# Filter products by a 52x128 block matrix in a two-layer spectral kernel, with new orders for its first two stages

## The chip, the cores and the metric

The kernel runs on one core of a Trainium2 chip. The core has TensorE (PE; its weight loads are PEld in the profile), VectorE (DVE), ScalarE (ACT) and GpSimd (POOL); SyncE (SP) issues nearly all of the DMAs, which sixteen DMA engines carry out. The metric is the device time of one launch in microseconds (us), the median of three runs.

## The reference, cut to what matters

Two layers; in each, a spectral mixing block and a feed-forward block are added to an image tensor of 8 images of 128 x 128 pixels with 96 channels. The mixing block, of which the change touches the filter part:

```
x_pre = relu(norm(x) @ w1.T) ** 2                       # 192 channels
xf    = rfft2(x_pre)                                    # 128 x 65 frequencies
filt[s] = Rh[s] @ cw[s] @ Rw[s].T                       # s = 3 scales: (16,9), (8,4), (24,13) -> (128,65), complex
comb  = sum_s softmax_s(gate(x)) * filt[s]              # an image's own mixture, for each channel
x     = x + irfft2(xf * comb) @ w2.T
```

`cw[s]` is real and imaginary, for 192 channels. Rw resizes along the width to 65 frequencies and Rh along the height to 128. Rw does not depend on the image, so its product is made once in each layer, by the code that is changed here.

## The kernel before, in words

**Work and stages.** Sixteen jobs (two layers of eight images) go through three pipelined stages, each in 16 steps for one image: P (`pixels`, 8 rows of pixels a step: norm, projection, squaring, transform along the width), F (`frequencies`, 4 width frequencies a step: transform along the height, filter, projection, inverse transform along the height) and S (`tokens`: inverse transform along the width, then the feed-forward block). P hands its result to F through the DRAM tensors `a_d`, F to S through `y_d`. F is 19 ticks behind P, S 19 behind F.

**Order.** The order of the work is written by hand. A tick goes through a table of entries (stage, step, how many items ahead), and each entry advances the generator of the stage by one `yield`. The order in the table is the program order on every engine. Ticks -5 to 14 use `RAMP` (P only), 15 to 35 `RISE` (P and F), 36 to 257 `TICK` (all three), then `FALL` and `TAIL`. For the P steps named here: 0 loads xt, 1 are the statistics (L491), 2 is the normalisation on GpSimd (L562), 3 the transposes pt_a (L566), 4 ScalarE's copy xT, 5 and 10 the projections pw0 and pw1 (L577), 6 and 11 ScalarE's r, 9 and 14 VectorE's sums sd (L595), 15 and 16 the width transforms pa0 and pa1 (L604), 17 to 20 ScalarE's lo, VectorE's at and the store to `a_d`. For the F steps: 0 loads al and ut, 1 is the filter times the image's mixture (L711, GpSimd), 2 to 4 are pf and px (L723, L739), 5 and 10 py (L757), 13 and 14 pz (L839, L847), 16 is pi (L863). N are the norm's small operations, G the gate of an image, which in RISE runs at ticks 16 and 17 for the first image and at 32 and 33 for the second.

**PSUM.** Five tags share the eight banks: d0, d1 and d2 are pairs of banks, s3 and s4 single ones. `RAMP_BANKS` and `RISE_BANKS` say which tile uses which tag in a stage. A tile waits until the one before it on its tag has been read.

**The filter products (U).** `load_filters` puts a layer's coefficients into `cw`: four blocks of 26 rows (9 + 4 + 13 width coefficients) at partitions 0, 32, 64 and 96, each for 48 channels, with 96 (real and imaginary, 48 heights) as the innermost dimension. `filters(i)` makes a group of 8 of the 96 heights: step 0 is four matmuls of 26 rows x 65 columns by 384, one in each 32-row quarter (L294), into ps_u (the pair d0) and ps_v (s3, s4); step 1 two copies on ScalarE (L307), step 2 two on VectorE (L309), step 3 a store to `u_d` (L314), which for each frequency writes a run of 8 x 192 fp32. There are 12 groups in a layer: layer 0 at ticks 3 to 14, layer 1 at ticks 21 to 32 (`UAHEAD`, `UPAUSE`). The moving operand is

```
cws[l][32 * i : 32 * i + NWS, :, n0 : n0 + UN].rearrange("p m n -> p n m")
```

which steps from channel to channel by 96 fp32. F reads `u_d` at its step 0 as ut, 112 rows of heights by 4 (or 5) frequencies.

**Background.** `background()` loads coefficients and weights, one piece a tick from tick 0, at the entry ("P", 9) of the table.

Of the kernel before, what the change touches and what calls it, by code (L numbers as in the profile page):

```python
# [1 line left out]

# [8 lines left out]
F32 = mybir.dt.float32  # L11
# [28 lines left out]
UM = 48  # L40
UN = 8
NU = NG // UN
# [3 lines left out]
EVENTS_AFTER = ("P", 9)  # L46
# [30 lines left out]
    ("U", 3, -1),    ("F", 7, 1), ("P", 1, 2), ("P", 0, 3), ("P", 13, -1), ("U", 0, 0), ("F", 12, 0),  # L77
    ("P", 3, 1), ("P", 5, 0), ("N", 0, 0), ("U", 1, 0), ("P", 4, 1), ("F", 13, 0),
    ("U", 2, 0), ("P", 14, -1), ("P", 6, 0), ("P", 15, -1), ("F", 8, 1), ("P", 16, -1),
    ("P", 17, -1), ("F", 14, 0), ("P", 7, 0), ("P", 18, -1), ("F", 9, 1), ("P", 8, 0),  # L80
    ("F", 10, 1), ("P", 19, -1), ("P", 20, -1), ("N", 1, 0), ("F", 15, 0), ("F", 11, 1),
    ("P", 9, 0), ("F", 0, 3), ("P", 10, 0), ("P", 11, 0), ("F", 16, 0), ("F", 1, 2),
    ("F", 2, 2), ("N", 2, 0), ("F", 3, 2), ("F", 17, 0), ("P", 12, 0), ("P", 2, 2),
    ("F", 4, 2), ("F", 5, 2), ("F", 18, 0), ("F", 6, 2),
# [3 lines left out]
    1: ((8, 0), (25, 1), (29, 2), (37, 3), (38, 4), (42, 5), (45, 6)),  # L88
    2: ((7, 7), (24, 8), (30, 9), (32, 10)),
# [14 lines left out]
    ("U", 3, -1), ("U", 0, 0), ("P", 0, 5), ("P", 13, 0), ("U", 1, 0), ("P", 20, -1), ("P", 7, 1),  # L104
    ("P", 1, 4), ("U", 2, 0), ("P", 3, 2), ("P", 4, 2), ("P", 8, 1), ("N", 1, -1),
    ("P", 14, 0), ("N", 0, 0), ("N", 2, -1), ("P", 2, 3), ("P", 9, 1), ("P", 10, 1),
    ("P", 15, 0), ("P", 11, 1), ("P", 16, 0), ("P", 17, 0), ("P", 18, 0), ("P", 19, 0),
    ("P", 5, 2), ("P", 12, 1), ("P", 6, 2),
# [12 lines left out]
    "pa0": 0, "pa1": 1, "pw0": 2, "pw1": 2, "pt_a": 1, "ps_u": 0, "ps_v0": 3, "ps_v1": 4,  # L121
# [8 lines left out]
    "ps_g": 3, "ph": 3, "pl": 3, "pa0": 2, "pa1": 0, "pw0": 0, "pw1": 2, "pt_a": 2,  # L130
    "pf0": 0, "pf1": 2, "py0": 1, "py1": 1, "pz0": 3, "pz1": 4, "pi0": 3, "pi1": 4,
    "px": 3, "pg": 3, "ps_u": 0, "ps_v0": 3, "ps_v1": 4,
# [35 lines left out]
def _constants():  # L168
# [48 lines left out]
    rw4 = np.zeros((128, NKW))  # L217
    for i in range(M // UM):
        rw4[32 * i : 32 * i + NWS] = rw
    made = dict(  # L220
        dft=f_w, fwd=np.stack(fwd, 1), inv=np.stack(inv, 1), idft=d, rh=rh2, rw=rw4,
# [18 lines left out]
def metaformer_kernel(ctx: ExitStack, tc: tile.TileContext, x, cst, layers, out):  # L240
# [33 lines left out]
    u_d = [dram.tile([NKW, GP, M], F32, name=f"u_d{l}") for l in range(len(layers))]  # L274
# [4 lines left out]
    def load_filters(l, p):  # L279

        cws[l] = us.tile([128, UM, NG], F32, name="cw")
        for i in range(M // UM):
            if l and i:
                yield
            nc.sync.dma_start(cws[l][32 * i : 32 * i + NWS], p["cw"][:, i * UM : (i + 1) * UM, :])

    def filters(i):

        l, n0 = i // NU, i % NU * UN
        pu = bank2("ps_u")  # L290
        pss = [pu[:NKW, i, : UN * UM] for i in range(2)]
        pss += [bank1(f"ps_v{i}")[:NKW, : UN * UM] for i in range(2)]
        for i in range(M // UM):
            mm(  # L294
                pss[i].rearrange("p (n m) -> p n m", m=UM),
                kt["rw"][32 * i : 32 * i + NWS],
                cws[l][32 * i : 32 * i + NWS, :, n0 : n0 + UN].rearrange("p m n -> p n m"),
                start=True,
                stop=True,
            )  # L300
        yield
        u = us.tile([NKW, UN, M], F32, name="u", bufs=3)
        uv = u.rearrange("p n (i m) -> p i n m", m=UM)
        for i, ps in enumerate(pss):
            o = ps.rearrange("p (n m) -> p n m", m=UM)
            if i < 2:
                nc.scalar.copy(uv[:, i], o)  # L307
            else:
# [784 lines left out]
```

## Time and profile before

| | |
|---|---|
| median of three runs | 4905.85 us (4905.08 to 4906.21) |
| profiled execution, its own time | 4904.48 us |
| its span, first to last instruction | 4901.7 us |
| granted TensorE clock, mean | 0.987 |
| start of the projection pw of tiles 0, 16, 32 | 20.84, 137.88, 391.92 us |
| ticks with U: ramp, rise (the usual one) | 7.33, 16.08 us |
| ticks without U: ramp, rise (the usual one) | 6.28, 14.32 us |
| DMA share: 50 to 137, 137 to 182, 196 to 392 us | 74%, 85%, 69% |
| L294, records and median | 192, 0.82 us |
| L307 (ScalarE), L309 (VectorE) | 48 x 0.48, 48 x 0.55 us |

A tick's length is read from TensorE's timeline, from one block of transposes (pt_a) to the next. A record's duration includes its way through the array, so the distance from one start to the next tells what a matmul costs, and not its duration. An fp32 matmul stands in the records twice. "Idle before" in square brackets names what ended the wait.

### The profile page before, as it was taken

What the parts mean: (1) busy time and instruction counts of PE and PEld (TensorE: products, weight loads), DVE (VectorE), ACT (ScalarE), POOL (GpSimd) and SP (SyncE); (2) the same over time, 40 slices, a digit from 0 to 9 for tenths busy, and PEclk for the clock granted to TensorE, in tenths of its full rate; (3) what the DMA queues carried; (4) which work ended last, traced back from release to release, by engine and by line L of the source; (5) the groups of instructions that cost most, each with busy time, mean ns of one, the idle gap of its engine ahead of it and who ended that gap; (6) DMA issues with size and microseconds to landing.
All of it is one profiled execution on the core that took longest, in us unless ns stands there. A gap on an engine that the chain in (4) does not pass through costs nothing.

```text
span 4901.7 us, 123978 instructions
## 1 busy us (share of the span) xinstructions
PE 4811.2 (98%) x44232; PEld 3752.2 (77%) x44232; DVE 4595.1 (94%) x13949; ACT 4314.8 (88%) x7104; POOL 2535.4 (52%) x1886
## 2 busy tenths in 40 slices
PE   8999999999999999999999999999999999999997
PEld 5677787777777777777877777777777777777764
DVE  8888999999999999999999999999999999998998
ACT  7555999999999999999999999999999999998987
POOL 4444555555555555555555555555555555554544
PEclk9999999999999999999999999999999999999997
DMA  6767777777777777777777777877777777776754
GB/s 196 206 188 210 206 215 214 215 212 216 212 213 215 217 215 214 213 214 215 216 213 215 213 216 212 219 213 213 213 214 214 212 219 213 214 215 180 207 169 125
DMA packets 917424, 1020.95 MB, mean 208 GB/s; under 512 B 75826, under 2 KB 848914, under 8 KB 916602
## 3 DMA queue, kind: packets, MB, share of 16 engines
q1 hardware_dynamic: 916810, 1013.04, 74.7%
q8 instruction: 352, 5.77, 0.5%
q14 instruction: 262, 2.15, 0.1%
HBM read 598.92 MB, written 413.84 MB: 207 GB/s over the span
## 4 chain that ended last, share of the span: by engine, by line
PE 89%; DVE 5%; ACT 4%; issue 1%; DMA 0%; POOL 0%; SPq 0%; POOLq 0%; DVEq 0%; ACTq 0%
PE pw L577 17%; PE py L757 14%; PE pz L847 9%; PE pf L723 7%; PE pa L604 7%; PE pi L863 7%; PE pm L942 6%; PE pz L839 5%; PE po L959 5%; PE pt_a L566 5%; PE ps_r L897 4%; PE pt_c L932 2%; DVE st L491 1%; ACT y L945 1%; ACT xn_c L918 1%
## 5 line engine op out<-in xcount | busy, mean ns | idle before, releaser
L800 POOL TENSOR_TENSOR xf<-pr 128x768 f32<-128x768 f32 x512 | 932.0, 1820 | 422.4 <-DVE pr L785 402.1
L577 PE MATMUL pw<-w,xT 97*128 97x240 f32 x4096 | 942.5, 373 | 6.1 <-DVE at L621 3.5
L757 PE MATMUL py<-k_fwd,al 128*128 128x128 f32 (+1 forms) x6208 | 801.8, 280 | 0.0
L945 ACT CAST y<-pm 128x1024 f16<-128x1024 f32 x768 | 754.4, 1017 | 42.0 <-PE pm L942 41.7
L577 PEld LDWEIGHTS pw<-w,xT 97*128 97x128 f32 x4096 | 741.4, 191 | 59.3 <-ACT r L580 10.9
L757 PEld LDWEIGHTS py<-k_fwd,al 128*128 128x128 f32 (+1 forms) x6208 | 744.6, 191 | 40.6 <-DVE pr L785 2.5
L952 ACT ACTIVATE h<-a 128x1024 fp8e5<-128x1024 f16 x729 | 773.3, 1061 | 0.2 <-DVE a L948 0.2
L589 POOL TENSOR_TENSOR acc<-acc,r 128x192 f32<-128x192 f32 x496 | 296.6, 598 | 919.0 <-ACT r L580 835.9
L977 POOL TENSOR_TENSOR y<-xr,o 128x768 f32<-128x768 f32 x256 | 422.2, 1649 | 671.4 <-DVE o L974 598.2
L580 ACT ACTIVATE r<-pw 128x960 f32<-128x960 f32 x512 | 497.3, 971 | 127.0 <-PE pw L577 127.0
L781 DVE TENSOR_TENSOR pr<-py,cf 128x768 f32<-128x768 f32 x512 | 488.1, 953 | 55.7 <-PE py L757 41.1
L595 DVE TENSOR_TENSOR sd<-xs 128x384 f32<-128x384 f32 x1008 | 522.8, 560 | 0.7 <-issue 0.3
L711 POOL TENSOR_TENSOR ut<-ut,rw 112x768 f32<-112x768 f32 (+1 forms) x256 | 473.3, 1849 | 41.0 <-DMA ut<-u_d 30.7
L723 PEld LDWEIGHTS pf<-k_rh,ut 48*128 48x128 f32 x6080 | 362.5, 189 | 149.2 <-issue 141.3
L942 PE MATMUL pm<-xq,f_q 96*128 96x512 fp8e5 x1536 | 432.1, 391 | 28.7 <-ACT y L945 22.7
L562 POOL TENSOR_TENSOR xn_a<-xt,n_rs 128x768 f32<-128x768 f32 x256 | 382.2, 1493 | 133.6 <-DVE n_rs L525 120.6
L935 ACT ACTIVATE xq<-pt_c 96x1024 fp8e5<-96x1024 f32 x256 | 261.2, 1020 | 202.0 <-PE pt_c L932 202.0
L583 ACT ACTIVATE xs<-r 128x768 f32<-128x768 f32 x512 | 436.8, 853 | 0.4
L723 PE MATMUL pf<-k_rh,ut 48*128 48x128 f32 x6080 | 412.0, 282 | 4.3 <-POOL ut L711 3.3
L918 ACT ACTIVATE xn_c<-xr,n_nb,n_rs 128x96 fp8e5<-128x96 f32 x1058 | 413.1, 487 | 0.0
L847 PE MATMUL pz<-w2c,xf 128*128 128x96 f32 x2048 | 396.6, 275 | 0.0
L764 ACT COPY cf<-pf 128x768 f32<-128x768 f32 x496 | 372.9, 801 | 26.6 <-PE pf L723 26.3
(133 smaller groups left out, 10173.6 us busy)
## 6 DMA issues: line engine op xcount, KB each, us to landing
a_d<-at SPq DMA_DIRECT2D x256, 768.0 KB
al<-a_d SPq DMA_DIRECT2D x1024, 192.0 KB
y_d<-yt SPq DMA_DIRECT2D x512, 192.0 KB
v<-y_d SPq DMA_DIRECT2D x256, 384.0 KB
ut<-u_d SPq DMA_DIRECT2D x256, 336.0 KB
xt<-in_x_dram SPq DMA_DIRECT2D x512, 96.0 KB
xr<-in_x_dram SPq DMA_DIRECT2D x256, 192.0 KB
mid<-y SPq DMA_DIRECT2D x256, 192.0 KB
```

Of the source, the lines that this page charges most:

```text
L577: mm(o, xT[:, 4 * a + 2 * i + j, :], wt["w1"], start=True, stop=True)
L580: nc.scalar.activation(r.rearrange("p a s c -> p a (s c)"), pw, AF.Relu)
L595: on.tensor_tensor(sd[:, e], xs[:, 0], xs[:, 1], op)
L711: nc.gpsimd.tensor_tensor(ut[:, -n:], ut[:, -n:], _bc_mid(jb.rw, n), ALU.mult)
L723: mm(pf[:, i, t * 128 : (t + 1) * 128], utf[64 * i : 64 * i + NHS, c0 : c0 + 128], kt["rh"][64 * i : 64 * i + NHS, :], start=True, stop=True,)
L757: mm(py[p0:p1, t, e, :], alf[:, e, c0 + p0 : c0 + p1], f, start=True, stop=True)
L781: nc.vector.tensor_tensor(p0, yv, crb, ALU.mult)
L800: nc.gpsimd.tensor_tensor(xf.rearrange("p t e f -> p (t e) f"), pr[:, 0].rearrange("p t r k -> p t (r k)"), pr[:, 1].rearrange("p t r k -> ...
L847: mm(pz[t][:, j, e, :], xf[:, 2 * t, e, :], wt["w2c" if t else "w2a"], start=False, stop=j == e == 1,)
L942: mm(pm[:, s, :], fk, xq[:, s, :], start=True, stop=True)
L945: nc.scalar.copy(y16, pm)
L952: nc.scalar.activation(hk, a16, AF.Copy, saturate=False)
```

## The change

- `cw` now holds 52 rows in each half of the partitions: the 26 rows of channels 0 to 95 and, below them, the 26 rows of channels 96 to 191. Both halves (partitions 0 to 51 and 64 to 115) hold the same coefficients, so each layer's coefficients are loaded twice. The constant rw becomes a block matrix: 52 x 128, of 2 x 64 frequencies.
- A group is 4 heights, real in the lower half and imaginary in the upper: two matmuls of 52 rows x 128 columns by 384, into ps_v0 and ps_v1; one copy on ScalarE, one on VectorE, both of 128 partitions; two stores of runs of 96 fp32. There are still 12 groups in a layer, in the same ticks.
- The 65th frequency (index 64) needs only the last coefficient of each scale. `load_filters` loads these in six pieces, transposes them (two transposes, one ScalarE copy) and stores them to `u_d`.
- `u_d` has 128 rows for each frequency, not 112.
- RAMP and RISE have new orders, banks and gate places; in RISE the xt loads are 4 ahead, not 3. The background starts at tick -3, at the entry ("P", 12); the weights of layer 1 are loaded two kinds at a time.

```diff
-UM = 48
-UN = 8
-NU = NG // UN
+UN = 4
+NU = NHS // UN
-EVENTS_AFTER = ("P", 9)
+EVENTS_AFTER = ("P", 12)
...
 RISE = (
-    ("U", 3, -1),    ("F", 7, 1), ("P", 1, 2), ("P", 0, 3), ("P", 13, -1), ("U", 0, 0), ("F", 12, 0),
-    ("P", 3, 1), ("P", 5, 0), ("N", 0, 0), ("U", 1, 0), ("P", 4, 1), ("F", 13, 0),
-    ("U", 2, 0), ("P", 14, -1), ("P", 6, 0), ("P", 15, -1), ("F", 8, 1), ("P", 16, -1),
-    ("P", 17, -1), ("F", 14, 0), ("P", 7, 0), ("P", 18, -1), ("F", 9, 1), ("P", 8, 0),
-    ("F", 10, 1), ("P", 19, -1), ("P", 20, -1), ("N", 1, 0), ("F", 15, 0), ("F", 11, 1),
-    ("P", 9, 0), ("F", 0, 3), ("P", 10, 0), ("P", 11, 0), ("F", 16, 0), ("F", 1, 2),
-    ("F", 2, 2), ("N", 2, 0), ("F", 3, 2), ("F", 17, 0), ("P", 12, 0), ("P", 2, 2),
-    ("F", 4, 2), ("F", 5, 2), ("F", 18, 0), ("F", 6, 2),
+    ("P", 1, 2), ("P", 13, -1), ("F", 12, 0), ("P", 14, -1), ("F", 7, 1), ("P", 3, 1),
+    ("N", 0, 0), ("P", 5, 0), ("P", 4, 1), ("P", 6, 0), ("U", 0, 0), ("U", 1, 0),
+    ("P", 15, -1), ("P", 16, -1), ("U", 2, 0), ("F", 13, 0), ("F", 8, 1), ("F", 14, 0),
+    ("P", 17, -1), ("P", 7, 0), ("U", 3, -1), ("F", 9, 1), ("P", 18, -1), ("P", 8, 0),
+    ("P", 19, -1), ("P", 20, -1), ("F", 0, 3), ("F", 10, 1), ("N", 1, 0), ("P", 0, 4),
+    ("F", 11, 1), ("P", 9, 0), ("F", 15, 0), ("P", 10, 0), ("N", 2, 0), ("F", 16, 0),
+    ("P", 11, 0), ("F", 1, 2), ("F", 2, 2), ("F", 17, 0), ("F", 3, 2), ("F", 18, 0),
+    ("P", 12, 0), ("P", 2, 2), ("F", 4, 2), ("F", 5, 2), ("F", 6, 2),
 )
 RISE_GATE = {
-    1: ((8, 0), (25, 1), (29, 2), (37, 3), (38, 4), (42, 5), (45, 6)),
-    2: ((7, 7), (24, 8), (30, 9), (32, 10)),
+    1: ((4, 0), (29, 1), (29, 2), (43, 3), (44, 4), (46, 5), (46, 6)),
+    2: ((16, 7), (28, 8), (30, 9), (33, 10)),
 }
...
 RAMP = (
-    ("U", 3, -1), ("U", 0, 0), ("P", 0, 5), ("P", 13, 0), ("U", 1, 0), ("P", 20, -1), ("P", 7, 1),
-    ("P", 1, 4), ("U", 2, 0), ("P", 3, 2), ("P", 4, 2), ("P", 8, 1), ("N", 1, -1),
-    ("P", 14, 0), ("N", 0, 0), ("N", 2, -1), ("P", 2, 3), ("P", 9, 1), ("P", 10, 1),
-    ("P", 15, 0), ("P", 11, 1), ("P", 16, 0), ("P", 17, 0), ("P", 18, 0), ("P", 19, 0),
-    ("P", 5, 2), ("P", 12, 1), ("P", 6, 2),
+    ("P", 19, -1), ("P", 0, 5), ("P", 13, 0), ("P", 1, 4), ("P", 7, 1), ("P", 20, -1),
+    ("N", 1, -1), ("P", 8, 1), ("N", 0, 0), ("P", 14, 0), ("N", 2, -1), ("P", 15, 0),
+    ("U", 0, 0), ("P", 3, 2), ("U", 1, 0), ("P", 4, 2), ("P", 9, 1), ("P", 10, 1),
+    ("P", 5, 2), ("P", 16, 0), ("P", 17, 0), ("P", 11, 1), ("P", 18, 0), ("U", 2, 0),
+    ("P", 12, 1), ("P", 6, 2), ("U", 3, 0), ("P", 2, 3),
 )
...
 RAMP_BANKS = {
-    "pa0": 0, "pa1": 1, "pw0": 2, "pw1": 2, "pt_a": 1, "ps_u": 0, "ps_v0": 3, "ps_v1": 4,
+    "pa0": 0, "pa1": 1, "pw0": 2, "pw1": 1, "pt_a": 2, "ps_v0": 4, "ps_v1": 3,
 }
 RISE_BANKS = {
-    "ps_g": 3, "ph": 3, "pl": 3, "pa0": 2, "pa1": 0, "pw0": 0, "pw1": 2, "pt_a": 2,
+    "ps_g": 4, "ph": 4, "pl": 3, "pa0": 2, "pa1": 0, "pw0": 0, "pw1": 2, "pt_a": 2,
...
-    "px": 3, "pg": 3, "ps_u": 0, "ps_v0": 3, "ps_v1": 4,
+    "px": 3, "pg": 4, "ps_v0": 3, "ps_v1": 4,
 }
...
-    rw4 = np.zeros((128, NKW))
-    for i in range(M // UM):
-        rw4[32 * i : 32 * i + NWS] = rw
+    rw2 = np.zeros((128, 128))
+    for h in range(2):
+        for i in range(2):
+            p = 64 * h + NWS * i
+            rw2[p : p + NWS, 64 * i : 64 * i + 64] = rw[:, :-1]
...
-    u_d = [dram.tile([NKW, GP, M], F32, name=f"u_d{l}") for l in range(len(layers))]
+    u_d = [dram.tile([NKW, 128, M], F32, name=f"u_d{l}") for l in range(len(layers))]
...
     def load_filters(l, p):
-        cws[l] = us.tile([128, UM, NG], F32, name="cw")
-        for i in range(M // UM):
-            if l and i:
+        cws[l] = us.tile([128, C, NG], F32, name="cw")
+        for i in range(2):
+            for h in range(2):
+                q = 64 * h + NWS * i
+                nc.sync.dma_start(cws[l][q : q + NWS], p["cw"][:, C * i : C * i + C, :])
                 yield
-            nc.sync.dma_start(cws[l][32 * i : 32 * i + NWS], p["cw"][:, i * UM : (i + 1) * UM, :])
+        last = us.tile([C, 2, NG], F32, name="cw_last")
+        h0 = w0 = 0
+        for h, w in SCALES:
+            w0 += w
+            to = last.rearrange("p u (r n) -> p u r n", r=2)[:, :, :, h0 : h0 + h]
+            end = p["cw"][w0 - 1].rearrange("(u p) (r n) -> p u r n", u=2, r=2)
+            for u in range(2):
+                nc.sync.dma_start(to[:, u], end[:, u, :, h0 : h0 + h])
+            h0 += h
+        yield
+        ps = bank1("ps_w")[:NG, :M]
+        for u in range(2):
+            nc.tensor.transpose(ps[:, u * C : (u + 1) * C], last[:, u], ident[:C, :C])
+        ends = us.tile([NG, M], F32, name="cw_end")
+        nc.scalar.copy(ends, ps)
+        yield
+        for r in range(2):
+            nc.sync.dma_start(u_d[l][NKW - 1, 64 * r : 64 * r + NHS, :], ends[NHS * r : NHS * r + NHS])
 
     def filters(i):
         l, n0 = i // NU, i % NU * UN
-        pu = bank2("ps_u")
-        pss = [pu[:NKW, i, : UN * UM] for i in range(2)]
-        pss += [bank1(f"ps_v{i}")[:NKW, : UN * UM] for i in range(2)]
-        for i in range(M // UM):
+        pss = [bank1(f"ps_v{h}")[:, : UN * C] for h in range(2)]
+        for h, ps in enumerate(pss):
+            q, n1 = slice(64 * h, 64 * h + 2 * NWS), NHS * h + n0
             mm(
-                pss[i].rearrange("p (n m) -> p n m", m=UM),
-                kt["rw"][32 * i : 32 * i + NWS],
-                cws[l][32 * i : 32 * i + NWS, :, n0 : n0 + UN].rearrange("p m n -> p n m"),
+                ps.rearrange("p (n m) -> p n m", m=C),
+                kt["rw"][q],
+                cws[l][q, :, n1 : n1 + UN].rearrange("p m n -> p n m"),
                 start=True,
                 stop=True,
             )
         yield
-        u = us.tile([NKW, UN, M], F32, name="u", bufs=3)
...
+        u = us.tile([128, 2, UN * C], F32, name="u", bufs=3)
+        nc.scalar.copy(u[:, 0], pss[0])
+        yield
+        nc.vector.tensor_copy(u[:, 1], pss[1])
+        yield
+        for b in range(2):
+            dst = u_d[l][:64, :, C * b : C * b + C].rearrange("k (h n) m -> k h n m", h=2)
+            nc.sync.dma_start(
+                dst[:, :, n0 : n0 + UN],
+                u[64 * b : 64 * b + 64].rearrange("p h (n m) -> p h n m", m=C),
+            )
         yield
...
     def background():
+        constants("rw")
         yield from load_filters(0, layers[0])
-        constants("rw")
-        yield
         yield from other_weights(0, layers[0])
...
         for k, _ in enumerate(token_weights(0, layers[0])):
-            if k >= 3:
+            if k >= 1:
                 next(cw1)
             yield
-        for _ in cw1:
-            yield
-        yield
+        yield from cw1
         yield from projection_weights(1, layers[1])
-        yield from other_weights(1, layers[1])
-        yield from token_weights(1, layers[1])
+        for _ in zip_longest(other_weights(1, layers[1]), token_weights(1, layers[1])):
+            yield
...
-        ud = u_d[jb.l].rearrange("k n m -> n k m")
+        ud = u_d[jb.l].rearrange("k n m -> n k m")[:GP]
...
-                    if t >= 0:
+                    if t >= -3:
                         next(events, None)
```

## The prediction

> **What bounds the kernel now.** I read the page's busy table first, then TensorE's and VectorE's timelines in the first 60 us and at 420 us, the table of stretches, the tile view of the filter products, and SyncE's waits. The page says that TensorE sets the time:
>
> ```profile
> PE 4811.2 (98%) x44232; PEld 3752.2 (77%) x44232; DVE 4595.1 (94%) x13949; ACT 4314.8 (88%) x7104; POOL 2535.4 (52%) x1886
> ```
>
> The change touches the two first stages only: the ramp (ticks -5 to 14, to about 138 us) and the rise (ticks 15 to 35, to about 455 us). The filter products (group U, L294) run at ticks 3 to 14 and 21 to 32, once each. TensorE's timeline, a ramp tick without U and one with it:
>
> ```profile
> 37.89 1.05 PE L566 MATMUL pt_a<-ident,xn_a 128*96 128x128 f32 x8 [0.42 <-DVE at L621]
> ...
> 44.17 1.05 PE L566 MATMUL pt_a<-ident,xn_a 128*96 128x128 f32 x8 [0.34 <-DVE at L621]
> 45.06 1.79 PE L577 MATMUL pw<-w,xT 97*128 97x240 f32 x8
> 46.77 1.52 PE L604 MATMUL pa<-sd,dft 64*64 64x384 f32 x16
> 48.23 1.89 PE L577 MATMUL pw<-w,xT 97*128 97x240 f32 x8
> 50.04 0.84 PE L294 MATMUL ps_u<-cw,k_rw 26*65 26x384 f32 x2
> 50.06 0.84 PE L294 MATMUL ps_v<-cw,k_rw 26*65 26x384 f32 x2
> 50.71 0.82 PE L294 MATMUL ps_u<-cw,k_rw 26*65 26x384 f32 x2
> 50.72 0.82 PE L294 MATMUL ps_v<-cw,k_rw 26*65 26x384 f32 x2
> 51.47 1.08 PE L566 MATMUL pt_a<-ident,xn_a 128*96 128x128 f32 x8
> ```
>
> Each fp32 matmul leaves two records, so a group's eight are four matmuls side by side: the second pass starts 0.67 us after the first, and the block holds TensorE 1.43 us (50.04 to 51.47). The table of stretches, two ramp ticks (without, with U) and two rise ticks (with, without U); after the length come PE, PEld, DVE, ACT, POOL busy, clock, DMA share:
>
> ```profile
> 37.89:44.17 6.28, 5.94 (x40) 4.20 (x41) 6.02 (x25) 5.51 (x11) 3.92 (x5) 1.00 0.81 234
> 51.47:58.80 7.33, 7.33 (x53) 4.41 (x49) 6.89 (x25) 6.25 (x12) 3.89 (x5) 1.00 0.64 204
> ...
> 211.43:227.51 16.08, 16.08 (x137) 12.11 (x133) 13.38 (x35) 9.30 (x17) 7.94 (x6) 1.00 0.45 133
> ...
> 422.36:436.68 14.32, 14.32 (x126) 11.87 (x125) 12.59 (x34) 8.44 (x15) 8.11 (x7) 1.00 0.85 236
> ```
>
> So U costs 1.05 us in a ramp tick (without it VectorE is the bound, TensorE idles 0.34 to 0.42) and 1.76 in a rise tick, where TensorE has no gap. All of U is worth 12 x 1.05 + 12 x 1.76 = 33.7 us: that caps the gain.
>
> **What the skill says.** Trainium skill, SBUF — State Buffer, section Door 1: an SBUF line is 16 bytes, and a stream reads at full rate only with two or more hits in a line, so fp32 may step by four elements at most. U's moving operand steps by 96 floats from element to element, before and after. The trace agrees: at the same 384 columns, pa (L604, contiguous, four tiles side by side) takes 1.45 us for four passes, some 0.33 us a pass, U takes 0.67, twice as long. TensorEngine Tiling (Array Packing), Key Properties, says that a change of tiling mode drains the array: py takes 1.44 us to the next start when pt_a follows in the same mode (420.92 to 422.36) and 1.53 when U does (208.47 to 210.00), so a switch costs 0.09; and pt_a and the pw after it together take 0.24 longer behind U. The forecast goes by the trace's sizes and the pages' reasons. The trace alone can't exclude that four row tiles at once make U slow, and not the stride; that is the first rival.
>
> **Part by part.**
>
> *The products.* Two 52-row matmuls take the place of four 26-row ones that already ran side by side. Columns (384) and stride are the same, so the passes are too: 2 x 0.66 = 1.32 us. Nothing is saved in the stream. Weights are 128 columns, not 65: the load rows are 0.19 (as pf's) and 0.13, +0.06 if exposed.
>
> *Order in the rise.* U stood between py and pt_a, two modes of its own (1.76 - 1.32 = 0.44 of switching and slower first records). It now stands between pw and pa, which switched anyway, in the same 64-row halves as pz and pf: one switch more, 0.09. So 1.32 + 0.06 + 0.09 = 1.47 for 1.76: -0.29 a tick, x12 = -3.5 us.
>
> *Order in the ramp.* pa1, pa0, U, pt_a, pw, pw: three switches instead of four, -0.1 to -0.2, against +0.06 of weights. 7.33 becomes about 7.2: x12 = -1.6. VectorE's tick without U is 6.28; two copies, 0.47 apart, made that 7.2, and one makes it 6.75, no longer close to TensorE. Three ticks from 70 to 94 us last 7.52, 7.97 and 8.22, where VectorE's memsets and TensorE's waits for it meet; with the room -1.
>
> *Evictions.* One ScalarE copy less (0.48) and one VectorE copy less (0.55) a group. In the rise they stood beside a full TensorE (VectorE 13.4 of 16.1): worth nothing. The pair of banks of ps_u is freed; no wait for it shows.
>
> *A new wait.* In the rise pw0 and pa1 share bank pair 0, and pa0, pa1 now follow pw0 with only U between. pa1 must wait for ScalarE's r: 0.97 us that begins 0.1 after pw0, against pa0's 0.73. With U (1.4) it is hidden; in the ticks without U it leaves 0.4 of a bubble, and pz, py and all of TensorE stand behind it. Six such full ticks (18 to 20, 33 to 35): +2.4.
>
> *The 65th frequency.* A layer: two transposes (0.11 each in pt_a), one 96x192 copy (0.3), six loads of short runs and two stores (SyncE 0.4 each, 3 us in three ticks). TensorE reaches the transposes a tick after the loads. Less than 1 us in all, put at 0; if the loads are later than a tick, some 2 us a layer.
>
> *DMA.* Each layer's filter coefficients are loaded twice, once for each row half: as much again as the 104 rows of 18.4 KB, which took 1.26 us each, so 104 x 1.26 / 16 = 8 us more of every engine in each layer. In layer 0 they go out from tick -3 in four pieces rather than in one burst at 25.8 us; in layer 1 at ticks 15 to 18, where the DMA share is 84% (137 to 182 us) and GpSimd waits 2.6 us for a ut's load (L711). Against that, al and ut are issued earlier in a tick, before the piece and before xt, where they stood behind both. SyncE: xt now stands behind F0's al and ut loads and the at store, but it is issued a tick earlier. At the change of stage the ticks' chains differ (the gate's steps move, xT before pa0 on one bank pair): I put +1, from -4 to +6, because idle TensorE there runs slower for a while (pa 2.84 us at 143.23 for 1.45).
> u's stores were 65 rows of 6 KB a group, 0.25 us each: 65 x 0.25 / 16 = 1.0 us of each engine. Now they are 1024 runs of 384 B. The trace has only loads of that size, 22 ns each: 1024 x 22 / 16 = 1.4 us, the lower bound; the upper is the second rival's. I take the row's 22, and then the stores are hidden: the DMA engines are 64% to 77% busy in these ticks.
>
> *Sum.* -3.5 - 1.6 - 1 + 2.4 + 1 = -2.7 us. The profiled execution took 4904.48 (span 4901.7, 2.8 around it), the median is 4905.85; both less 2.7 gives 4901.8 and 4903.1. Forecast 4903. From tick 36 on nothing is changed but u_d's row pitch; that part, nine tenths of the time, stays.
>
> **Rivals.**
>
> *Four tiles, not the stride, made U slow.* Then two tiles run at pa's rate, 0.66 for two passes instead of 1.32: rise -0.66 x 12 = -7.9; ramp only to VectorE's 6.75, -0.45 x 12 = -5.4. 4903 - 13.3 = 4890. For it: no other strided operand is in the trace to compare. Against it: the factor is two, just what one hit a line for two gives, and pa too has more than one tile.
>
> *The ramp becomes bound by the stores (slower).* Trainium skill, DMA: Bandwidth & Descriptors, Specifications: below 512 B a transfer is a read-modify-write. No run here shows its price. In the ramp the stores of at and the loads of xt take 3.65 us of each engine a tick (128 x 292 ns and 512 x 41 ns, over 16), the constants 0.75; of a 7.2 us tick 2.8 is left: 44 ns a run is the point from which it decides. The 768 B rows reach 60 to 70 when crowded; at 65 the runs take 4.2 us, and the twelve ticks 1.4 more each (3.65 + 0.75 + 4.2 = 8.6 for 7.2), +17. With the ramp's gain gone: 4922. In the rise (69% of 16 us busy) 3 us more still fit. Three buffers of u give three ticks of delay before ScalarE's copy waits.
>
> *A worse order than I see* at the change of stage, where each idle spell also slows TensorE: +6 beyond the sum, 4909, still within what counts as no change.
>
> **How the numbers follow.** 0.2% is 9.8 us, about what a measurement of this kernel can tell from no change. Stride stays the limit and the DMA hides: 0.66, at 4903, its own range 4895 to 4911 (the change of stage -4 to +6, the three ticks, the weights); I leave it 0.12 of this beyond -9.8 and 0.06 beyond +9.8. Full rate: 0.16, 4890. Stores bind or loads of the second layer hold the rise up: 0.18, 4912 to 4925. Faster 0.08 + 0.15 = 0.23, rounded to 0.25; slower 0.04 + 0.16 = 0.20, to 0.22; the rest 0.53. The range takes in the full-rate case and most of the slow one: 4887 to 4918.
>
> **What would show it.** Right: U's passes still 0.66 apart; a block of about 1.4 us; ramp ticks with U 7.1 to 7.25, TensorE without gap; rise ticks with U 15.7 to 15.9; those without U 14.6 to 14.8 with a gap before pa that ScalarE's r ends; the end of the rise about 3 us earlier. Wrong: passes 0.33 apart (the first rival); ScalarE's u copies waiting for u's stores, VectorE for xt, the DMA share near 1 in the ramp (the second); or a different tick after 455 us, which none of the steps explains.

## The result, and the profile after

| | before | changed |
|---|---|---|
| median of 13 runs each, the same chip | 4906.41 us (4903.09 to 4911.13) | 4917.36 us (4914.37 to 4920.56) |
| profiled execution, its own time | 4904.48 us | 4918.25 us |
| its span, granted clock | 4901.7 us, 0.987 | 4916.2 us, 0.986 |

The ratio is 1.0022, with a 95% interval from 1.0015 to 1.003: the change costs 11 us. The forecast was 4903, three microseconds less than before. The time lies inside the range that was given (to 4918), but in the case "slower by over 0.2%", which had a chance of 0.22.

TensorE is still the busiest engine, and its busy time is as before within 1.1 us:

```profile
PE 4812.3 (98%) x44140; PEld 3756.1 (76%) x44140; DVE 4591.5 (93%) x13925; ACT 4306.3 (88%) x7082; POOL 2532.5 (52%) x1886
```

So the 11 us are not more work for TensorE; the stretches below show where it idles and where it runs slower. To find the place I took the start of each tile's first width transform (pa) from both traces and subtracted. The difference stays at 12.1 us from tile 38 to tile 60 and is 12.0 at the last tile: from about 500 us on nothing is slower in sum. (The last 420 us, after the last pa, are the same code in every kernel here and took between 418.2 and 425.1 in the profiled executions, with no pattern. Spans therefore differ by up to 7 us for no reason that this study looks at, and stretches are compared instead.) What lies ahead of tile 60:

| stretch, by pa's start | before | changed | difference | by ticks | the forecast's steps |
|---|---|---|---|---|---|
| up to tile 0 (tick 0) | 34.13 | 31.84 | -2.3 | +0.8 | not treated |
| tiles 0 to 5 (ticks 0 to 5): the first ticks of the ramp | 34.62 | 40.20 | +5.6 | +6.5 | nothing but shorter U ticks |
| tiles 5 to 14 (ticks 5 to 14): the rest of the ramp | 67.68 | 65.78 | -1.9 | -1.9 | -1.6 and -1, over twelve ticks |
| tiles 14 to 19 (ticks 14 to 20): the change of stage | 62.81 | 72.25 | +9.4 | +6.4 | +1, and +0.4 for each tick without U |
| tiles 19 to 31 (ticks 20 to 32): rise with U | 195.56 | 193.90 | -1.7 | -1.5 | -3.5 |
| tiles 31 to 35 (ticks 32 to 36): the last U tick, then rise without U | 63.64 | 66.47 | +2.8 | +1.9 | +1.2 |
| tiles 35 to 60 (ticks 36 to 61) | 458.16 | 458.30 | +0.1 | -0.2 | 0 |

**Where the cut falls.** pa's start is not the same point of the work in the two orders. In a tick of the old ramp, U, pt_a and pw1 stand ahead of pa0; in the new ramp pa0 stands ahead of them. At tile 14 the changed kernel therefore still has a U (1.47 us), a pt_a (0.9) and a pw (1.7) to do that the kernel before has behind it, and at tile 19 only the first pz (1.06). Some 3 of the 9.4 us are this, and not a loss. The column "by ticks" has the difference from the first TensorE instruction of a tick's table to that of another's; a tick's table holds the same TensorE steps in both orders, so up to there both kernels have done the same work. Everything said of the change of stage across the two orders goes by this column: it takes 69.66 us for 63.21, 6.4 more.

The table of stretches for ticks 0 to 3 and 14 to 20, before and changed in turn, says how the time is lost:

```profile
31.03:50.04 19.01, 18.00 (x121) 12.57 (x119) 17.09 (x63) 16.67 (x30) 11.48 (x13) 1.00 0.75 205
31.84:57.65 25.81, 21.21 (x124) 15.10 (x123) 18.28 (x70) 16.82 (x30) 11.21 (x12) 0.87 0.75 176
132.38:195.59 63.21, 53.56 (x390) 40.64 (x390) 48.83 (x152) 35.66 (x63) 27.84 (x25) 0.89 0.79 193
137.82:207.48 69.66, 58.98 (x388) 44.32 (x381) 49.08 (x149) 35.46 (x63) 26.13 (x24) 0.80 0.93 226
```

After the length come PE's busy time and, in the third place from the end, its granted clock. Of the 6.8 us lost in ticks 0 to 3, TensorE idles 3.6 longer and is busy 3.2 longer with the same work, at a clock of 0.87 for 1.00. At the change of stage it idles only 1.0 longer and is busy 5.4 longer, at 0.80 for 0.89. So of these 13.2 us the larger part, 8.6, is TensorE running slower and the smaller part is idle time. In the whole run this doesn't show, because its busy time is shorter elsewhere (by 2.9 us in ticks 20 to 32 alone).

**The steady ticks** are near where the forecast put them. This is TensorE's timeline of the changed kernel, a ramp tick:

```profile
111.35 1.08 PE L581 MATMUL pt_a<-ident,xn_a 128*96 128x128 f32 x8
112.27 3.41 PE L592 MATMUL pw<-w,xT 97*128 97x240 f32 x16
115.61 1.52 PE L619 MATMUL pa<-sd,dft 64*64 64x384 f32 x16
117.06 1.54 PE L314 MATMUL ps_v<-cw,k_rw 52*128 52x384 f32 x4
118.53 1.08 PE L581 MATMUL pt_a<-ident,xn_a 128*96 128x128 f32 x8
```

U's block takes 1.47 us (117.06 to 118.53), near what the four small matmuls took (1.43), and the tick is 7.18 us (111.35 to 118.53). The table of stretches shows this ramp tick from pa on, then a rise tick with U and one without:

```profile
113.89:121.06 7.17, 7.17 (x45) 4.59 (x44) 6.92 (x24) 6.04 (x12) 3.89 (x4) 1.00 0.85 257
239.80:255.59 15.79, 15.79 (x130) 12.17 (x129) 12.85 (x34) 8.92 (x16) 7.93 (x7) 1.00 0.81 209
434.61:449.48 14.87, 14.55 (x127) 11.77 (x126) 12.51 (x33) 8.32 (x15) 8.10 (x7) 1.00 0.68 178
```

The first two have no gap in TensorE. The third has 0.32 us of it, and TensorE's timeline names the place: between the two pa of a tile, and it is ScalarE's r that ends it, as the forecast said of pa1.

```profile
436.32 0.88 PE L619 MATMUL pa<-sd,dft 64*64 64x384 f32 x8
437.51 0.88 PE L619 MATMUL pa<-sd,dft 64*64 64x384 f32 x8 [0.32 <-ACT r L595]
438.32 1.14 PE L854 MATMUL pz<-w2b,xf 64*128 64x96 f32 x16
```

In the kernel before the two pa stand in one block:

```profile
426.02 1.52 PE L604 MATMUL pa<-sd,dft 64*64 64x384 f32 x16
427.47 0.46 PE L847 MATMUL pz<-w2a,xf 128*128 128x96 f32 x2
```

From the first pa to the pz behind them it is 2.00 us, for 1.45: all of the 0.55 that the tick is longer (14.87 for 14.32) lies here.

**The start.** From tile 1 to tile 2 the changed kernel takes 12.89 us, the kernel before 6.28. The chain of waits of the changed kernel (start, length, what) runs through two DMAs there:

```profile
17.75 13.16 DMA cw<-in_L_cw_dram
...
30.93 10.48 DMA xt<-in_x_dram
...
41.51 0.72 DVE st L506 x4
...
44.07 6.44 PE pw L592 x16
```

A coefficient load issued at 17.75 lands 13.16 us later. SyncE waits for that before it issues the next piece of a tile's pixels (xt, at 30.93), which takes 10.48 us to land behind another such load. VectorE's statistics start on it at 41.51, its copies of at stand behind them, and TensorE's pw, which waits for these, then runs at a granted clock of 0.54 (6.44 us; 3.4 in the steady ticks). The table of waits (total, times, longest) shows the same twice, for VectorE and for SyncE's queue:

```profile
DVE st L506 <- DMA xt<-in_x_dram: 13.4, 4, 6.0
```

```profile
SPq L567 <- DMA cw<-in_L_cw_dram: 13.6, 3, 5.7
```

In the kernel before, VectorE has no wait for xt there, and SyncE's only waits for cw are short (1.2 and 0.7) and in front of other transfers:

```profile
SPq L624 <- DMA cw<-in_L_cw_dram: 1.2, 1, 1.2
```

From 14 to 50 us the DMA table gives the queue's share of the 16 engines as 86.3% in the changed kernel and 63.8% before. The bytes, 6.48 MB for 6.11, differ by only 6%, because other transfers have been pushed out of the stretch (16 issues of xt for 24). By size, the 104 rows of coefficients of layer 0 take 2.98 us each, 19.4 us of every engine, for 1.37 us and 8.9 before (layer 1: 18.7 for 7.5). The last of them ends at 46.6 us.

**The change of stage.** Here the chain of the changed kernel is again made of DMAs:

```profile
152.27 8.41 DMA a_d<-at
...
164.03 4.42 DMA xt<-in_x_dram
168.45 1.78 POOL ut L726
170.27 2.93 PE pf L738 x24
...
180.56 3.88 issue
...
184.48 1.88 POOL ut L726
186.40 2.80 PE pf L738 x24
```

The store of at that ends the first image takes 8.41 us (before: issued at 147.70, followed by al at 152.04, so 4.3). Its landing releases the loads al (L720) and ut (L722); GpSimd's product (ut) follows, and only then TensorE has pf. But this is not where most is lost. Counted from tick 14's start, the first product begins at 30.6 us (before 29.0), the second at 46.7 (42.5), the third at 61.6 (55.0). In front of the second, GpSimd waits for the load of its own ut, issued at 172.46, 4.7 us behind a coefficient load. The table of waits has the longest such wait in the changed kernel and before:

```profile
POOL ut L726 <- DMA ut<-u_d: 3.9, 1, 3.9
```

```profile
POOL ut L711 <- DMA ut<-u_d: 2.6, 1, 2.6
```

The pf behind these waits take 2.93 and 2.80 us (1.54 in the steady ticks). From 137 to 182 us the DMA queue's share is 88.8%; before, it was 84.3%.

### The profile page after: what moved, and what is told of

Its sections match the earlier page's. It is cut to its first block, busy times and chain, and to the rows that moved or that the text cites. A ratio compares the mean times of both kernels' runs of the same rounds, so it can differ in the third digit from the quotient of the medians.

```text
span 4916.2 us, 123757 instructions
## 1 busy us (share of the span) xinstructions
PE 4812.3 (98%) x44140; PEld 3756.1 (76%) x44140; DVE 4591.5 (93%) x13925; ACT 4306.3 (88%) x7082; POOL 2532.5 (52%) x1886
## 4 chain that ended last, share of the span: by engine, by line
PE 87%; DVE 5%; ACT 3%; DMA 2%; issue 1%; POOL 1%; SPq 1%; POOLq 0%; DVEq 0%; ACTq 0%
PE pw L592 16%; PE py L772 14%; PE pz L862 9%; PE pf L738 7%; PE pa L619 7%; PE pi L878 7%; PE pm L957 6%; PE pz L854 5%; PE po L974 5%; PE pt_a L581 4%; PE ps_r L912 4%; PE pt_c L947 2%; DVE st L506 1%; ACT y L960 1%; ACT xn_c L933 1%
## 5 line engine op out<-in xcount | busy, mean ns | idle before, releaser
L610 DVE TENSOR_TENSOR sd<-xs 128x384 f32<-128x384 f32 x1008 | 538.3, 576 | 0.3 <-PE pw L592 0.3
L619 PE MATMUL pa<-sd,dft 64*64 64x384 f32 x4096 | 394.2, 497 | 4.6 <-ACT r L595 2.5
```

Of the source, the lines that this page charges most:

```text
L610: on.tensor_tensor(sd[:, e], xs[:, 0], xs[:, 1], op)
L619: mm(pa[64 * e : 64 * e + 64, p].rearrange("q (s m) -> q s m", m=M), wt["dft"][64 * p : 64 * p + 64, 64 * e : 64 * e + 64], sd[64 * p : 64 ...
```

## The experiments

Each was run in five rounds with the kernel before on the same chip, to which its ratio refers (before's median there was between 4904.6 and 4905.0). The stretches are read from the one profiled execution of each kernel, by pa's start as in the table above; the last column is the change of stage by ticks, the only one to compare across the two orders:

| kernel | median, us | ratio, 95% interval | tiles 0 to 14 | 14 to 19 | 19 to 60 | ticks 14 to 20 |
|---|---|---|---|---|---|---|
| before | 4906.41 | | 102.30 | 62.81 | 717.35 | 63.21 |
| changed | 4917.36 | 1.0022 [1.0015, 1.0030] | 105.98 | 72.25 | 718.67 | 69.66 |
| changed, half the coefficients | 4906.56 | 1.0002 [0.9994, 1.0010] | 99.61 | 66.15 | 718.60 | 63.56 |
| before, 75% more coefficients | 4913.17 | 1.0017 [1.0010, 1.0023] | 111.48 | 65.57 | 714.55 | 65.97 |
| changed, short rows | 4917.19 | 1.0024 [1.0014, 1.0034] | 103.62 | 72.29 | 717.82 | 69.70 |
| changed, loads in pairs | 4927.85 | 1.0047 [1.0034, 1.0061] | 108.69 | 78.41 | 719.76 | 75.40 |
| changed, order of before | 4922.97 | 1.0035 [1.0021, 1.0049] | 106.64 | 68.20 | 731.05 | 68.61 |
| changed, contiguous | 4894.62 | 0.9980 [0.9971, 0.9988] | 94.11 | 67.10 | 708.69 | 64.51 |
| before, contiguous | 4894.09 | 0.9975 [0.9965, 0.9984] | 98.73 | 62.53 | 710.98 | 62.33 |
| changed, contiguous, order of before | 4895.67 | 0.9981 [0.9973, 0.9989] | 98.34 | 63.42 | 705.29 | 63.77 |
| changed, padding early | 4914.96 | 1.0020 [1.0011, 1.0029] | 103.39 | 72.13 | 722.53 | 69.54 |
| contiguous, padding early | 4894.49 | 0.9975 [0.9965, 0.9985] | 94.56 | 66.82 | 709.19 | 64.23 |
| the same, loads a tick later | 4896.44 | 0.9981 [0.9974, 0.9989] | 94.61 | 66.08 | 712.91 | 63.49 |

### Half the coefficients

Each half of the partitions multiplies only its own 48 heights, real or imaginary. This kernel loads only those.

```diff
-nc.sync.dma_start(cws[l][q : q + NWS], p["cw"][:, C * i : C * i + C, :])
+own = slice(NHS * h, NHS * h + NHS)
+nc.sync.dma_start(cws[l][q : q + NWS, :, own], p["cw"][:, C * i : C * i + C, own])
```

> Each half of cw loads only the columns its own products read (real in the lower, imaginary in the upper): half the bytes, in runs of 192 B instead of rows of 36.9 KB; the loads stand at the same places. Theory, bytes of the doubled loads hold up xt at the start and at and ut at the change of stage: the tick of 12.9 us at the start falls to about 6.5, the stretch between pw of tile 16 and of tile 20 loses some 7 us, 4917 becomes 4902 to 4906. Rival, the new order itself or the earlier place of the loads makes these gaps: at most 5 us come back, 4912 to 4917. In both, ticks with U stay at 7.17 and 15.79.

Measured: 4906.56, 10.8 us less than the changed kernel and no different from before. The start's loss is gone: the tick from tile 1 to tile 2 takes 6.43 us for 12.89, and SyncE has no wait for cw left. The change of stage keeps 0.4 of its 6.4 us by ticks (3.3 of 9.4 by pa's start, of which 3 are where the cut falls). There too the first store of at takes 7.1 us; what has gone is the delay at the second and third product (43.5 and 56.9 us from tick 14's start). The loads are now runs of 192 B at 25.0 ns, 15.6 us of every engine for 19.4, so engine time fell less than the bytes; the last run still ends 9 us earlier, at 37.5 us for 46.6. The doubled coefficient bytes cost the changed kernel nearly all of its loss. In ticks 14 to 20 TensorE idles 12.2 us here, more than in the changed kernel (10.7), but is busy 51.3 for 59.0, at a granted clock of 0.92: what the loads cost there comes as slower running. Why the clock falls further with them is not shown; idle time in sum does not explain it.

### Before, with more coefficients

The other direction, in the old order and with the old products: behind each load of 48 channels goes one of 36 channels into a tile that nothing reads.

```diff
+again = us.tile([128, UA, NG], F32, name="cw_again")
-nc.sync.dma_start(cws[l][32 * i : 32 * i + NWS], p["cw"][:, i * UM : (i + 1) * UM, :])
+for to, n in (cws[l], UM), (again, UA):
+    nc.sync.dma_start(to[32 * i : 32 * i + NWS], p["cw"][:, i * UM : i * UM + n, :])
```

> The kernel before with 75% more coefficient bytes: each of the eight loads is followed by one of 36 of the 48 channels into a tile that nobody reads. Bytes theory: xt is late by some 6 us after the burst at 26 us, and the change of stage grows by 2 to 6; 4905 becomes 4910 to 4918. Order theory (the bytes cost nothing in the old order): 4904 to 4907.

Measured: 4913.17, 8.5 us more than before on that chip (4904.62). The ramp loses 9.2 us, all of it by tile 4, and the change of stage 2.8. The chain at the start is the one seen above:

```profile
27.04 11.35 DMA cw_again<-in_L_cw_dram
...
38.40 11.41 DMA xt<-in_x_dram
...
49.90 0.28 DVE st L494 x2
```

Three quarters of the bytes that the change adds cost the kernel before 8.5 us, where the change as a whole costs 11, without any of its products or orders. Its split is another one, though: more at the start and less at the change of stage.

### Short rows, and loads in pairs

Two kernels ask what it is about these loads. In the first each load is cut into four of 24 channels:

```diff
-nc.sync.dma_start(cws[l][q : q + NWS], p["cw"][:, C * i : C * i + C, :])
+for c0 in range(0, C, C // 4):
+    part = slice(c0, c0 + C // 4)
+    src = p["cw"][:, C * i + c0 : C * i + c0 + C // 4, :]
+    nc.sync.dma_start(cws[l][q : q + NWS, part], src)
```

> The changed kernel with each coefficient load of 936 KB cut into four loads of 24 channels: the same bytes at the same entry of the order, rows of 9.2 KB for 36.9 KB, and twelve SyncE issues more in each layer. It asks whether the length of the rows makes xt and at wait, or the bytes. Theory (the bytes): the rows take about 0.72 us each, a quarter of 2.93, still 19 us an engine in each layer; the ticks of tiles 1 and 2 stay near 19 us together (before 13.6), the stretch from tile 14 to tile 19 near 72 us (before 62.8); 4915 to 4921. Rival (a long row holds a queue up): the start loses less than 2 us to the kernel before and the change of stage less than 7 of its 9.4; 4908 to 4912.

Measured: 4917.19, the change of stage 72.29. A row takes 0.73 us and the rows together 18.9 us of every engine. VectorE still waits for xt,

```profile
DVE st L509 <- DMA xt<-in_x_dram: 11.1, 4, 5.3
```

and tiles 1 to 3 take 17.2 us for the changed kernel's 19.4 and the earlier 13.6. So the start loses 3.6 us, between what the theory (near 5.4) and the rival (under 2) expected, and the change of stage all it lost before. It is in the main the bytes ahead of xt; the length of a row is at most the smaller part of the start's loss.

In the second the loads for the lower and the upper partitions go out together, in two of the four ticks:

```diff
             nc.sync.dma_start(cws[l][q : q + NWS], p["cw"][:, C * i : C * i + C, :])
-            yield
+        yield
+        yield
```

> The changed kernel with the loads for the lower and the upper half of the partitions issued together, in two ticks of the four instead of one load in each: bytes, rows and number of loads are the same. Trainium skill, SBUF - State Buffer, section Door 1: The DMA port swizzle, says that a load reaches only the ports of its partitions, 26 partitions below 32 at most 8 of 16, and that the other half has ports of its own. If the ports bound the loads (theory), a pair of loads lands about as soon as one does now, so all four have landed by 36 us, for 46.6 in the changed kernel, and tiles 1 and 2 take 13.5 to 16 us together for 19.2: 4910 to 4914. If the loads are bound by what all queues share, or by their place in front of xt (rival), a pair holds xt up for twice as long: tiles 1 and 2 take 18 to 22 us, the change of stage 72 to 76, and the time is 4916 to 4923.

Measured: 4927.85, above even the rival's bounds. Tiles 1 to 3 take 21.9 us, the change of stage 78.4. The loads as a whole end little earlier (42.9 us for 46.6), and one xt waits longer:

```profile
15.04 13.24 DMA cw<-in_L_cw_dram
...
31.20 13.91 DMA xt<-in_x_dram
```

The Trainium skill, SBUF — State Buffer, section Door 1, ties a load's bandwidth to the ports that its partitions reach, and the two halves have ports of their own. If that bounded these loads, pairs would have landed by about 36 us. They don't. That so much lies ahead of one tile's pixels at a time fits the longer wait of xt; it is not shown apart from the rest.

### The order of before

The changed products and loads, with RAMP, RISE, their banks and gate places as they were before (the background stays at tick -3 and at the entry ("P", 12)).

```diff
-RAMP = (("P", 19, -1), ("P", 0, 5), ("P", 13, 0), ...
+RAMP = (("U", 3, -1), ("U", 0, 0), ("P", 0, 5), ...
-RISE = (("P", 1, 2), ("P", 13, -1), ("F", 12, 0), ...
+RISE = (("U", 3, -1), ("F", 7, 1), ("P", 1, 2), ...
```

> The new products, loads and background with the RAMP and RISE tables, their gates and banks of before. Theory, bytes: the gaps at the start and at the change of stage stay; ticks with U become 7.3 and 16.0, those without U in the rise 14.3 instead of 14.87; 4917 to 4923. Rival, the order makes the gaps: the stretch of the change of stage falls by 7 or more, 4906 to 4911.

Measured: 4922.97. U ticks are 7.37 (ramp) and 15.93 (rise), those without U 14.32: the new order is worth 0.2 and 0.14 on a tick with U and costs 0.55 on one without. The step for the rise had put its whole 0.29 down to the order; half of it comes with the products in the old order (15.93 for 16.08). The start still loses (tick of tile 1: 9.01). The change of stage loses 5.4 to before; with the new order it is 6.4, so the order is about 1 us of it (by pa's start the difference would read 4.1). The 13.7 us more in tiles 19 to 60 are this mixture's own: the ticks from tiles 24, 25, 30 and 31 (22.8, 20.8, 20.9 and 18.3 us), in a mixture of old order and new background that neither kernel has; the chain there runs through a load of al and through U's waits for VectorE, and it was not taken apart. Its total therefore says little; its ticks do.

### Contiguous coefficients

The host lays the coefficients out with the channels innermost, so that U's moving operand steps by 1 and not by 96. This is done to the changed kernel (each half is then loaded once, in rows of 18.4 KB, and the 65th frequency comes by six loads without transposes) and to the kernel before, four small matmuls and all.

```diff
-cws[l][q, :, n1 : n1 + UN].rearrange("p m n -> p n m"),
+cws[l][q, n0 : n0 + UN],
```

> The coefficients are given in the order in which the products read them (halves of channels, real and imaginary, heights, channels innermost): each half is loaded once, in rows of 18.4 KB, the moving operand steps by one element, and the 65th frequency needs no transposes. Bytes theory and stride theory: U's passes 0.33 us apart instead of 0.66, ticks with U 6.7 to 6.8 in the ramp (VectorE the bound) and 15.1 in the rise, gaps gone: 4917 - 13 - 5 - 8 = 4891 (4887 to 4896). If the stride costs nothing: passes stay at 0.66, 4902 to 4906. If bytes are not the cause of the gaps: 4900 to 4905 with passes at 0.33.

> The kernel before with the coefficients given with channels innermost: four matmuls side by side as before, the moving operand steps by one element instead of 96. Stride theory: passes 0.33 apart, rise ticks with U 16.08 - 0.66 = 15.4, ramp ticks 7.2 (VectorE's two copies bind), 4906 - 8 - 2 = 4896 (4893 to 4900). Rival, four row tiles at once are the limit: passes stay at 0.66, 4905 to 4908.

Measured: 4894.62 and 4894.09, both faster than before, by 0.20% and 0.25%. The groups of U's matmuls by shape (busy time, then mean ns of one) in the kernel before and in it with contiguous coefficients,

```profile
L294 PE MATMUL ps_u<-cw,k_rw 26*65 26x384 f32 x96 | 35.6, 824 | 1.4 <-DVE at L621 1.4
```

```profile
L294 PE MATMUL ps_u<-cw,k_rw 26*65 26x384 f32 x96 | 20.7, 506 | 2.6 <-DVE at L621 2.1 <-issue 0.5
```

and in the changed kernel without and with them:

```profile
L314 PE MATMUL ps_v<-cw,k_rw 52*128 52x384 f32 x96 | 37.0, 853 | 0.0
```

```profile
L308 PE MATMUL ps_v<-cw,k_rw 52*128 52x384 f32 x96 | 22.0, 535 | 0.0
```

A record is 0.32 us shorter in both. On the timeline, where starts count and not durations, the second pass begins 0.38 us after the first in the kernel before (0.67 with the stride) and 0.43 in the changed one (0.72), 0.29 less in both, and a whole block of U is 0.85 us (1.43 and 1.47). Four row tiles side by side gain as much as two: it is the stride, at least between the two steps tried, 96 and 1, and not the number of tiles. The rise tick becomes 15.17 in the changed kernel and 15.46 in the one before, the ramp tick 6.55 to 7.19 and 6.72, below the 7.2 that VectorE's two copies were expected to set. The block matrix is worth 0.3 us a rise tick over four small matmuls, products and order together, and loses it again at the change of stage (by ticks 64.5 for 62.3) and in the ticks without U.

### Contiguous, with the order of before

By pa's start the contiguous changed kernel is 4.6 us longer there than the contiguous kernel before; by ticks it is 2.2. Is that the order's, or the products' and their loads'? This kernel is the contiguous changed one with RAMP, RISE, banks, gate places and the background's entry ("P", 9) of before.

> The contiguous kernel (coefficients loaded once a half, operand with step 1, 65th frequency loaded directly) with the orders, banks and gate places of the kernel before, and the background at (P, 9) again, still from tick -3. It asks whether the new order or the products and their loads make the change of stage long: from pa of tile 14 to pa of tile 19 the kernel before took 62.8 us, before with contiguous coefficients 62.5, the contiguous kernel with the new order 67.1. Theory (the new order costs there): 62 to 63.5 us here, but ramp U ticks some 0.2 longer than with the new order (6.75 to 6.9), rise U ticks 15.3 to 15.4 for 15.17, and ticks without U back at 14.3: in all 4890 to 4894. Rival (the loads cost there, 10 us an engine in layer 1): 66 to 67 us stay, the U ticks are the same as above, in all 4894 to 4899.

Measured: 4895.67, somewhat over what was expected. By pa's start the change of stage takes 63.4 us for 67.1, as the theory had it, but 2.4 of these 3.7 us are where the cut falls (a U of 0.85, a pt_a and a pw, less a pz). By ticks it is 63.8 for 64.5: the new order costs 0.7 us there, and products and loads 1.4 over the contiguous kernel before (62.3). In the trace the store of at now lands in 5.8 us (7.7 with the new order), and GpSimd's product waits for its own ut:

```profile
143.57 5.82 DMA a_d<-at
...
152.03 5.56 DMA ut<-u_d
```

In the ramp the new order gains: up to tick 14 it is 1.6 us ahead (126.9 us for 128.5). In the last ticks of the rise, which wait for r, it loses 2.4.

### Padding early, loads late

I had suspected the zeros that `padding` stores at tick 13, in front of the change of stage, and then the coefficients of layer 1. Three kernels moved them:

```diff
 constants("rw")
 yield from load_filters(0, layers[0])
 yield from other_weights(0, layers[0])
+padding(0)
+yield
...
-padding(0)
-yield
...
-            if k >= 1:
+            if k >= 2:
```

> The changed kernel, with the one store of zeros to u_d (780 KB) at tick 3 instead of tick 13; the doubled loads stay. Theory, the zeros and the second layer's loads together fill the DMA engines at the change of stage: the stretch from pw of tile 16 to pw of tile 20 (65.8 us now) loses 3 to 4, 4917 becomes 4913 to 4915. Rival, only the doubled loads count there: no change, 4916 to 4919.

> The contiguous kernel (each half loaded once, rows of 18.4 KB) with the zeros at tick 3. If what is left of the gap at the change of stage (a tick of 20.6) is the store of at queued behind the zeros and u's stores: it falls to 14 to 17, 4894.6 becomes 4889 to 4892. If it is the new order's own chain: 4893 to 4896.

> As the one before, and the four coefficient loads of layer 1 one tick later, so that none stands ahead of the last at store of the first image. DMA theory: another 1 to 2.5 us, 4887 to 4891. Order theory: same as the one before.

Measured: 4914.96, 4894.49 and 4896.44. The padding is not it: with it early the change of stage stays at 72.13 (72.25) in the changed kernel and 66.82 (67.10) in the contiguous one. The first of the three has a median of 4914.96, within what the theory expected, but its stretch is the rival's; that the median is 2.4 us below the changed kernel, with intervals that overlap, I don't count. Loads one tick later take another 0.7 us from the stage (66.08), and the store of at lands in 3.3 us, but the ticks from tiles 26, 31 and 32 give back 3.9. By ticks the change of stage is then 63.5, 0.3 over the kernel before: little of the new order is left to be found there.

## Why the prediction was right or wrong

**Right in the main: what TensorE does.** "U's passes still 0.66 apart; a block of about 1.4 us" (1.47), "ramp ticks with U 7.1 to 7.25" (7.17), "rise ticks with U 15.7 to 15.9" (15.79) and "those without U 14.6 to 14.8 with a gap before pa that ScalarE's r ends" (14.87, the gap 0.32) came out or nearly so: 14.87 is just above its range, and the changed kernel's passes are 0.72 apart. That the new wait hits the ticks without U was found from the banks and the order alone. The sign "the end of the rise about 3 us earlier" did not come: it is 12.4 later. And VectorE waits for xt, which was put down as a sign of stores that bind, but it waits because of the loads.

**Right: the stride.** The first rival, four tiles as the reason for U's pace, is refuted twice: two tiles don't run faster (853 ns a record for 824), and four tiles run as fast as two once the step is 1. The Trainium skill, SBUF — State Buffer, section Door 1, lets fp32 step by four elements at full rate; the traces here have passes 0.67 and 0.72 us apart at a step of 96, and 0.38 and 0.43 at a step of one. That is a factor of about 1.7, where the prediction had taken two (0.33).

**Right: the stores.** u's 384 B runs took 24.5 ns in the ramp (66 to 140 us), by the estimate 22, and not the 44 from which the second rival decides. Neither ScalarE's nor VectorE's copy of u waits for a store there. The rule that the rival leaned on (DMA: Bandwidth & Descriptors, Specifications, a read-modify-write below 512 B) is not seen as a price here.

**Partly right: the rise.** The usual tick gains 0.29, but the ticks from tiles 19, 24 and 25 lose 1.05, 0.66 and 0.82, so twelve U ticks gain 1.7 for 3.5. The last four ticks lose 1.9 by ticks for 1.2: the wait costs 0.55 a tick, not 0.4. (By pa's start they lose 2.8, of which 1.06 is a pz on the other side of the cut.) The loss of 0.6 from tile 31 on, and those at tiles 19, 24 and 25, no experiment took apart.

**Wrong: the DMA step.** "Each layer's filter coefficients are loaded twice ... 8 us more of every engine in each layer" was worked out from rows at 1.26 us, and it is 10.5 in layer 0 (19.4 for 8.9) and 11.2 in layer 1 (18.7 for 7.5). What failed is the sentence after it: +1, from -4 to +6, at the change of stage, and nothing at the start, where it only noted that the loads go out in four pieces and not in one burst. Measured are +6.6 on the tick from tile 1 to tile 2, and +6.4 by ticks (+9.4 by pa's start) at the change of stage; in the kernel with half the coefficients both are nearly gone. Two things were missed at the start. The loads' price is set here by what needs to land next, not by a mean share: xt is issued by the same queue, and SyncE waits for a coefficient load's landing before the next xt goes out (13.6 us in three waits). And spreading over four ticks put a load in front of four tiles' pixels, which did not save them with loads of this size; before, fifteen pieces of xt had been issued (12.02 to 25.82 us) ahead of the one burst, and the first ticks had what they needed. With more bytes that place doesn't save the burst either, as the kernel with 75% more coefficients shows. At the change of stage the same holds of ut, which lies behind a coefficient load while GpSimd waits for it. The prediction had said that each idle spell slows TensorE there, within its +1; the slower running is the larger part, 5.4 of the 6.4 us, and 3.2 of the 6.8 in ticks 0 to 3.

**Not the cause: the order at the change of stage.** The third rival put +6 beyond the sum there. By ticks the order is 0.4 us of the 6.4 (what the half-coefficient kernel keeps, with the new products), 0.7 (the two contiguous kernels) and 1.1 (the order of before); the loads are 5.4 to 6.1. By pa's start it would seem 3.3 to 4.1, but 2.4 to 3 of that is the cut.

**The rival on the other side** had the right sign and nearly the right number (4922) for a wrong reason: the stores, which are hidden, and not the loads.

## What to carry to other kernels

A duplicated load is costed by the transfer that stands behind it on the queue and by the engine that waits for that one; where a tile is loaded only a tick or two ahead, a load of most of a megabyte in front of it was time on the path here, though the queue was busy only 64% before. Where the granted clock falls, busy time is to be read beside idle time: here it grew by more. Two orders of the same work are to be compared between points at which both have done the same; a tile's landmark moves with the order. A restructured product is worth what limits it: here the operand's stride set the pace, so a better fill of the array made no pass shorter, and a change of layout on the host gave the kernel before 0.25% without any other edit.

## What the hardware showed unexpectedly

- For the same matmuls TensorE was busy 59.0 us for 53.6 at the change of stage, at a granted clock of 0.80 for 0.89; the pw behind the wait at the start took 6.44 us for 3.4, at 0.54.
- Two loads of 936 KB issued together delayed what followed more than the same two in turn (tiles 1 to 3: 21.9 us for 19.4), although all four were through 3.7 us earlier.
- Cutting rows of 36.9 KB to 9.2 KB left their engine time nearly as it was (19.4 and 18.9 us): 12.4 and 12.7 KB per us and row, for 13.4 in rows of 18.4 KB before.
- Runs of 384 B into DRAM took 24.5 ns and loads in runs of 192 B 25.0 ns: half the bytes in runs that short saved a fifth of the engine time, and still all of the wait.
